# One tile shape for scores, projections and turns in a masked attention kernel: even key chunks, a padding row, and the output matmuls together

## The chip, the cores and the metric

The kernel runs on one core of a Trainium2 chip. The metric is the device time of one execution in microseconds (us), the median of several runs. The profile comes from one further execution; its span runs from the first to the last recorded instruction. Engines are called PE (TensorE, matrix products), ACT (ScalarE), DVE (VectorE), POOL (GpSimd) and SP (SyncE, which issues transfers here). Each engine and each queue works through its instructions in the order in which the program gives them.

## The reference

```python
def _L0_cond_ref(x, mask, Wq, Wo):          # x (8, 512, 1024), mask (8, 1024) of 0 and 1
    B, D, T = x.shape                       # NH = 8 heads, dk = 64
    xt = jnp.transpose(x, (0, 2, 1))
    q = xt @ Wq.T
    qh = q.reshape(B, T, NH, dk).transpose(0, 2, 1, 3)
    scores = scale * jnp.einsum('bhqd,bhkd->bhqk', qh, qh)   # queries are keys and values too
    logits = (scores * cmask + (1.0 - cmask) * NEG) * rmask
    attn = jax.nn.softmax(logits, axis=-1)
    ctx = jnp.einsum('bhqk,bhkd->bhqd', attn, qh)
    out = ctx.transpose(0, 2, 1, 3).reshape(B, T, D) @ Wo.T
    return jnp.transpose(out, (0, 2, 1))

x = x + _L0_cond_ref(x, cond_2048, Wq, Wo)
```

A masked key gets no weight. A masked query has all logits 0, so its context is the mean of all values, the same for every such query of a batch.

## The kernel before

Everything is fp32. `early()` counts the kept tokens of each batch and ranks them. If every batch keeps fewer than `NK` = 576 of its 1024 tokens, `late()` runs on the kept tokens alone; it is what the profile shows. `attention_of_all_tokens` is the way out for other inputs and does not run.

For each of 8 batches the tokens are turned to rows and stored in DRAM (`turn`, tile `xd`), a search over the ranks finds the rows of the kept ones (`search`), POOL gathers them in five tiles of up to 128 rows (`gather`, tile `xin`), and PE turns them back to feature-major columns (`collect`, tile `xc`, 512 features in `ND` = 4 blocks of 128 by 576 columns). The last column holds the batch's mean (`put_mean`), which stands for all masked queries.

The work then goes by *pairs* of heads: 4 pairs a batch, 32 in all, numbered p = 4 b + pr. For a pair: `project` makes the queries `qT` (128 rows, 64 a head) in two halves of 288 tokens; `values` turns them into `v`, squares them on ACT and reduces to a bound on the scores (`top`, then `bias_of`); `scores(pair, c)` makes, for key chunk c, the products of 128 keys with two halves of 288 queries and two heads, each head on its own 64 rows of the array, and ACT's exponential puts them in `e`; `add_up` sums each row of `e` over the valid columns on DVE, one masked reduction for each head (queries and keys are the same vectors, so a key's row sum is the softmax sum of that token as a query); `attend` multiplies `v` with `e` over the keys, into `av`, which ACT copies to `cT`; `invert`, a store and a broadcast load (`row`, `rb`, on SP) and `contexts` divide by the sums. 576 tokens are four key chunks of 128 and one of 64; for that last chunk the four products (two heads, two query halves) lie on four tiles of 64 x 64, and its sums come in two parts that `sum_last` adds. `output` multiplies four pairs' `cT` with `woT`, five token tiles a batch, ACT copies, POOL stores to `od`; `fetch` gathers rows of `od` back to the places of all tokens (8 indirect transfers on POOL), and `finish_blocks` turns them on DVE and adds `x`, which `load_rest` has loaded. SP stores the result. The last batch goes a shorter way (`begin_output`, `end_output`, `fetch_last`, `finish_tokens`).

The order is written out by hand. In pair p the loop runs over five chunks: `scores`, then the previous chunk's `add_up`, then whatever `slots_of` and the tables name for that pair and chunk: the projection of pair p + 2 in two lumps of 8 matmuls, the bias of pair p + 1, the values of pair p + 2 in the last slot, the outputs of the previous batch in slots 0 to 2 of pair 1, the mean and `collect` in slots 1 to 3 of pair 2. `attend` follows the loop. POOL's order within a steady batch is: output stores (pair 1, slots 0 to 2), five gathers (pair 1, slot 3), eight fetches (pair 2, slot 0). Eight of the features' sums for the mean stand on ACT in the chunks of pairs 0 and 1 (`add_features`).

PSUM tiles rotate: score tiles `s` of two banks, two of them, and tiles `t` of one bank, four of them (`bank`), for everything else. A new tile waits until the one that it replaces has been read.

Of the kernel before, what the change touches and what calls it, by code (L numbers as in the profile page):

```python
# [28 lines left out]

# [289 lines left out]
def attention_of_kept_tokens(ctx, tc, x, mask, wq, wo, out, ident, wqT, woT, verdict, flag):  # L319

# [36 lines left out]
    sizes = [min(P, NK - c * P) for c in range(-(-NK // P))]  # L357
    NC = len(sizes)
    LAST = NC - 1
    assert sizes[LAST] == DK == P // 2  # L360
    W = NC * P

# [5 lines left out]
    count = keep.tile([P, NK], F32, name="count")  # L368
    quadrant = keep.tile([P, A], F32, name="quadrant")
    within = keep.tile([P, Q], F32, name="within")  # L370
    key = keep.tile([P, NC], F32, name="key")
    kept = keep.tile([P, B], F32, name="kept")
    origin = keep.tile([P, B, NT], I32, name="origin")
# [3 lines left out]
    pens = keep.tile([P, B, NC], F32, name="pens")  # L377
    low = keep.tile([P, 2, LAST], F32, name="low")
    lowest = keep.tile([P, DK], F32, name="lowest")
    sums = [keep.tile([P, 2, NC], F32, name=f"sums_{i}") for i in range(2)]  # L380
    ris = [keep.tile([P, Q], F32, name=f"ris_{i}") for i in range(2)]
    ranks = dr.tile([B * NT, P], F32, name="ranks", bufs=1)

    def bank(name):
        return ps.tile([P, NB], F32, tag="t", name=name, bufs=4)
# [3 lines left out]
    xs, xbars, xmeans, xds, xins, xcs, valids, searches = {}, {}, {}, {}, {}, {}, {}, {}  # L389
# [13 lines left out]
    def queries_of(b):  # L403

        valid = sb.tile([P, NK], F32, tag="valid", name=f"valid_{b}")
        nc.gpsimd.tensor_scalar(valid, count, kept[:, b : b + 1], None, ALU.is_lt)  # L406
        part = sb.tile([P, KH], F32, tag="part", name=f"part_{b}")
        for r in range(2):
            rows = slice(r * DK, (r + 1) * DK)
            nc.gpsimd.tensor_copy(part[rows, :], valid[rows, r * KH : (r + 1) * KH])  # L410
        valids[b] = valid, part

    def turn_first(i):

        r, at = divmod(i * P, NB)
        pt = bank(f"xt_0_{i}")
        for d in range(ND):
            nc.tensor.transpose(pt[:, d * P : (d + 1) * P], xs[0][r][:, d, at : at + P], ident)  # L418
        if i == 0:
            xds[0] = dr.tile([T, D], F32, tag="xd", name="xd_0")  # L420
        tag = "oc" if i < NC else "xin"
        xt = sb.tile([P, D], F32, tag=tag, name=f"xt_0_{i}", bufs=NC)
# [11 lines left out]
    def turn(b, i):  # L434

        n = T // NQ
        r, at = divmod(i * n, NB)
        if i == 0:
            xds[b] = dr.tile([T, D], F32, tag="xd", name=f"xd_{b}")
# [34 lines left out]
    def place_ranks(b):  # L480
        rank = sb.tile([P, T], F32, tag="rank", name=f"rank_{b}", bufs=1)
        found = sb.tile([P, NC], F32, tag="found", name=f"found_{b}")
        source = sb.tile([P, NC], I32, tag="source", name=f"source_{b}")
        searches[b] = rank, found, source
# [8 lines left out]
    def search(b, i):  # L493

# [11 lines left out]
            source[:, col], found[:, col], float(i * P), float(T - 1), ALU.add, ALU.min  # L506
        )

    def gather(b, i):
# [3 lines left out]
        xin = sb.tile([P, D], F32, tag="xin", name=f"xin_{b}_{i}", bufs=NC)  # L513
# [8 lines left out]
    def collect(b, i):  # L522
        n = sizes[i]
        xin = xins[b][i]
        pt = bank(f"xc_{b}_{i}")
        for d in range(ND):
            nc.tensor.transpose(  # L527
                pt[:, d * n : (d + 1) * n], xin[:n, d * P : (d + 1) * P], ident[:n, :n]
            )
        m = min(n, NK - 1 - i * P)  # L530
        nc.scalar.copy(
            xcs[b][:, :, i * P : i * P + m],
            pt[:, : ND * n].rearrange("p (d n) -> p d n", d=ND)[:, :, :m],
        )

    def put_mean(b):

        xcs[b] = sb.tile([P, ND, NK], F32, tag="xc", name=f"xc_{b}", bufs=1)
        pm = bank(f"mean_{b}")
        for d in range(ND):  # L540
            nc.tensor.matmul(
                pm[d * Q : (d + 1) * Q, :A], within, xmeans[b][:, d, :], start=True, stop=True
            )
        nc.vector.tensor_scalar(xcs[b][:, :, NK - 1], pm[:, :A], 1.0 / T, None, ALU.mult)


    qTs, vs, tops, biases = {}, {}, {}, {}

    def project(pair, hf):
        b, pr = pair  # L550
        nm = f"{b}_{pr}"
        if hf == 0:
            qTs[pair] = sb.tile([P, W], F32, tag="qT", name=f"qT_{nm}", bufs=4)
        qT = qTs[pair]
        cols = slice(hf * KH, (hf + 1) * KH)
        pq = bank(f"pq_{nm}_{hf}")
        for d in range(ND):
            nc.tensor.matmul(  # L558
                pq[:, :KH],
                wqT[:, d, pr * P : (pr + 1) * P],  # L560
                xcs[b][:, d, cols],
                start=(d == 0),
                stop=(d == ND - 1),
            )
        nc.scalar.copy(qT[:, cols], pq[:, :KH])  # L565
        if hf == 1:
            nc.scalar.copy(qT[:, NK:W], pq[:, KH - DK : KH])

    def values(pair):
        nm = "%d_%d" % pair  # L570
        qT = qTs[pair]
        v = sb.tile([P, NC, P], F32, tag="v", name=f"v_{nm}", bufs=4)
        for at, n in ((0, LAST), (LAST, 1)):
            pt = bank(f"v_{nm}_{at}")
            for i in range(n):
                c = at + i
                nc.tensor.transpose(  # L577
                    pt[:, i * P : (i + 1) * P], qT[:, c * P : (c + 1) * P], ident
                )
            nc.scalar.copy(  # L580
                v[:, at : at + n, :], pt[:, : n * P].rearrange("p (c d) -> p c d", d=P)
            )
        vs[pair] = v
        sq = sb.tile([P, NC, P], F32, tag="sq", name=f"sq_{nm}", bufs=1)
        nc.scalar.activation(sq, v, AF.Square)  # L585
        lengths = sb.tile([P, 2 * NC], F32, tag="len", name=f"len_{nm}")
        nc.vector.tensor_reduce(  # L587
            lengths,
            sq.rearrange("p c (h d) -> p (c h) d", h=2),
            axis=AX.X,  # L590
            op=ALU.add,
        )
        tops[pair] = sb.tile([P, 1], F32, tag="top", name=f"top_{nm}")
        nc.vector.tensor_reduce(tops[pair], lengths, axis=AX.X, op=ALU.max)

    def bias_of(pair):
# [3 lines left out]
        nc.tensor.transpose(pt[:, :P], tops.pop(pair).to_broadcast([P, P]), ident)  # L600
        m = sb.tile([P, 1], F32, tag="m", name=f"m_{b}_{pr}")
        nc.vector.tensor_reduce(m, pt[:, :P], axis=AX.X, op=ALU.max)
        nc.vector.tensor_scalar(m, m, -SCALE, None, ALU.mult)  # L603
        biases[pair] = sb.tile([P, NC], F32, tag="bias", name=f"bias_{b}_{pr}")
        nc.vector.tensor_scalar(biases[pair], pens[:, b, :], m, None, ALU.add)

# [3 lines left out]
    def scores(pair, c):  # L610
        qT, nm = qTs[pair], "%d_%d_%d" % (*pair, c)
        heads = [slice(h * DK, (h + 1) * DK) for h in range(2)]
        keys = slice(c * P, c * P + sizes[c])
        if c < LAST:
            e = sb.tile([P, 2, 2, KH], F32, tag="e", name=f"e_{nm}", bufs=6)
        else:
            e = sb.tile([P, 1, 2, KH], F32, tag="el", name=f"el_{nm}")
            s = ps.tile([P, 2, NB], F32, tag="s", name=f"s_{nm}")
        for hf in range(2):
            queries = slice(hf * KH, (hf + 1) * KH)  # L620
            to = slice(0, P)
            if c < LAST:
                s = ps.tile([P, 2, NB], F32, tag="s", name=f"s_{nm}_{hf}")
            else:
                to = slice(hf * DK, (hf + 1) * DK)
            for h in range(2):
                nc.tensor.matmul(  # L627
                    s[to, h, :KH], qT[heads[h], keys], qT[heads[h], queries], start=True, stop=True
                )
            if c < LAST or hf == 1:  # L630
                nc.scalar.activation(  # L631
                    e[:, hf if c < LAST else 0, :, :],
                    s[:, :, :KH],
                    AF.Exp,
                    bias=biases[pair][:, c : c + 1],
                    scale=SCALE,
                )
        es[pair, c] = e

    def add_up(pair, c):  # L640

        b, pr = pair
        valid, part = valids[b]
        e = es[pair, c]
        for h in range(2):
            junk = sb.tile([P, T], F32, tag="junk", name=f"junk_{b}_{pr}_{c}_{h}", bufs=1)
            n = NK if c < LAST else KH
            nc.vector.tensor_tensor_reduce(  # L648
                junk[:, :n].rearrange("p (f k) -> p f k", k=KH),
                e[:, :, h, :],  # L650
                (valid if c < LAST else part).rearrange("p (f k) -> p f k", k=KH),
                1.0,
                0.0,
                ALU.mult,
                ALU.add,
                sums[pr % 2][:, h, c : c + 1],
            )

    def weigh(pair, av, c, hf):
        v, e = vs[pair], es[pair, c]  # L660
# [630 lines left out]
```

## Time and profile before

| what | us |
|---|---|
| median of 3 runs (807.15 to 809.01) | 807.57 |
| span of the profiled execution | 724.6 |
| first score starts, in the span | 37.0 |
| steady batch (batches 2 to 6) | 82.96 |
| last pair starts, in the span | 665.2 |
| last batch's tail, from the last output product's end to the end of the span | about 25 |
| ACT busy in the span | 384.1 |
| DVE busy in the span | 542.0 |
| POOL busy in the span | 171.9 |

The profiled execution's own time is its span and what lies around it; the runs differ from the span by 83.0 us (807.57 - 724.6), which is outside all recorded instructions. PE's mean granted clock is 0.98 of full speed. In the profile's rows, "128\*64" behind a matmul is the part of the array that it takes (rows\*columns), the rest are shapes of its operands; one fp32 product is two MATMUL instructions. "<-" names what ended an engine's idle time.

### The profile page before, as it was taken

To read this page: it belongs to the slowest core of one execution; us is meant where nothing else is said; L and a number is where in the kernel's file an instruction comes from. 1 tells how busy PE (TensorE), PEld (TensorE's weight loads), DVE (VectorE), ACT (ScalarE), POOL (GpSimd) and SP (SyncE) were. 2 spreads that over 40 slices of the span, in tenths; PEclk is the share of its full clock that TensorE was granted. 3 is DMA by queue.
4 is the path that set the end of the run, shared out by engine and by line. 5 is a ranking of instruction groups with operands and counts; after the bars stand their busy time and mean duration, and the time that the engine had idled before them with its cause. 6 is when DMAs were issued, how large, how long until landed. Compare 5 with 4: busy or idle time off the path is not lost.

```text
span 724.6 us, 11742 instructions
## 1 busy us (share of the span) xinstructions
PE 673.4 (93%) x4027; PEld 378.0 (52%) x4027; DVE 542.0 (75%) x1568; ACT 384.1 (53%) x763; POOL 171.9 (24%) x208
## 2 busy tenths in 40 slices
PE   6699999999999999999999999999999999998973
PEld 5555555555554555546554555455554555554332
DVE  6269967758986799858986699858988598637862
ACT  5476567455654556445664657445673645445300
POOL 4721000062102601054101701044100710023021
PEclk9899999999999999999999999999999999999985
DMA  8544152772579636783579634785468821754238
GB/s 292 157 150 129 56 164 64 185 196 93 181 199 234 201 96 181 209 207 124 164 193 229 200 125 142 206 222 152 164 169 199 215 88 41 167 132 131 59 113 248
DMA packets 96405, 117.35 MB, mean 162 GB/s; under 512 B 10080, under 2 KB 73632, under 8 KB 96336
## 3 DMA queue, kind: packets, MB, share of 16 engines
q1 hardware_dynamic: 79584, 74.14, 38.9%
q0 software_dynamic: 12528, 40.28, 17.8%
q10 hardware_dynamic: 4224, 2.10, 1.0%
q8 instruction: 33, 0.54, 0.3%
q14 instruction: 36, 0.29, 0.1%
HBM read 73.30 MB, written 43.18 MB: 161 GB/s over the span
## 4 chain that ended last, share of the span: by engine, by line
PE 82%; DVE 7%; ACT 6%; DMA 3%; issue 2%; POOL 0%; SPq 0%; DVEq 0%; POOLq 0%
PE av L664 19%; PE s L627 19%; PE pq L558 17%; PE po L777 15%; ACT e L631 4%; PE v L577 3%; PE xc L527 2%; DVE junk L648 2%; PE pa L797 2%; DVE junk L502 1%; DMA g<-od,origin 1%; PE xt L418 1%; DMA rb<-row 1%; PE po L813 1%; PE top L600 0%
## 5 line engine op out<-in xcount | busy, mean ns | idle before, releaser
L648 DVE CUSTOM_DVE_ANT_0 junk<-e,valid 128x576 f32<-128x576 f32 x256 | 193.5, 756 | 68.3 <-ACT e L631 61.3
L627 PE MATMUL s<-qT 64*128 64x288 f32 (+1 forms) x1280 | 186.7, 434 | 16.9 <-ACT e L631 16.7
L631 ACT ACTIVATE e<-s,bias 128x576 f32<-128x576 f32 x256 | 175.5, 737 | 20.4 <-PE s L627 17.2
L627 PEld LDWEIGHTS s<-qT 64*128 64x128 f32 (+1 forms) x1280 | 91.7, 174 | 103.9 <-ACT e L631 50.2
L558 PE MATMUL pq<-xc,wqT 128*128 128x288 f32 x512 | 140.4, 418 | 0.0
L664 PE MATMUL av<-e,v 128*64 128x288 f32 x1024 | 135.8, 411 | 0.1
L558 PEld LDWEIGHTS pq<-xc,wqT 128*128 128x128 f32 x512 | 92.2, 190 | 40.9 <-ACT cT L680 8.5
L777 PE MATMUL po<-woT,cT 128*128 128x512 f32 (+1 forms) x336 | 113.4, 525 | 0.0
L664 PEld LDWEIGHTS av<-e,v 128*64 128x64 f32 x1024 | 69.6, 136 | 55.0 <-ACT v L580 8.3
L786 POOL DMA_DIRECT2D od<-oc x42 | 23.4, 557 | 276.0 <-ACT oc L784 276.0
L777 PEld LDWEIGHTS po<-woT,cT 128*128 128x128 f32 (+1 forms) x336 | 48.9, 172 | 56.0 <-issue 51.5
L680 ACT COPY cT<-av 128x288 f32<-128x288 f32 x62 | 21.7, 402 | 97.7 <-PE av L664 97.7
L879 POOL DMA_INDIRECT g<-od,block_origin x56 | 62.1, 1109 | 19.0 <-issue 14.3
L784 ACT COPY oc<-po 128x512 f32<-128x512 f32 (+1 forms) x35 | 19.0, 543 | 87.0 <-PE po L777 85.7
L565 ACT COPY qT<-pq 128x288 f32<-128x288 f32 x64 | 25.5, 398 | 63.8 <-PE pq L558 63.8
L514 POOL DMA_INDIRECT xin<-xd,source x40 | 42.4, 1060 | 43.8 <-DVE m L603 25.6
L406 POOL TENSOR_SCALAR valid<-count,kept 128x576 f32<-128x576 f32 x8 | 14.1, 1762 | 130.3 <-DVE sums L648 130.2
L447 DVE STREAM_TRANSPOSE xt<-x 128x1024 f32<-128x1024 f32 x28 | 34.7, 1240 | 11.0 <-DMA xd<-xt 10.9
L587 DVE TENSOR_REDUCE len<-sq 128x10 f32<-128x640 f32 x32 | 25.8, 806 | 21.3 <-ACT sq L585 21.3
L502 DVE TENSOR_SCALAR_CACHE_REDUCE junk<-rank,key 128x1024 f32<-128x1024 f32 (+4 forms) x40 | 39.7, 994 | 1.5 <-ACT rank L1046 1.5
L849 DVE TENSOR_TENSOR xr<-o,xr 128x512 f32<-128x512 f32 x56 | 38.8, 692 | 1.9
L846 DVE STREAM_TRANSPOSE o<-g 128x512 f32<-128x512 f32 x56 | 39.3, 701 | 0.0
(139 smaller groups left out, 630.5 us busy)
## 6 DMA issues: line engine op xcount, KB each, us to landing
x<-in_x_dram SPq DMA_DIRECT2D x56, 256.0 KB
xd<-xt SPq DMA_DIRECT2D x112, 128.0 KB
xr<-in_x_dram SPq DMA_DIRECT2D x28, 512.0 KB
out_dram<-xr SPq DMA_DIRECT2D x24, 512.0 KB
rb<-row SPq DMA_DIRECT2D x60, 160.0 KB
od<-oc POOLq DMA_DIRECT2D x28, 256.0 KB, 4.0
rank<-ranks SPq DMA_DIRECT2D x6, 512.0 KB
xd<-xt POOLq DMA_DIRECT2D x8, 256.0 KB, 3.8
```

Source lines behind the costliest of these rows:

```text
L447: nc.vector.transpose(xt.rearrange("p k (d f) -> p k d f", d=ND), xs[b][r][:, :, at : at + n].rearrange("p d (k t) -> p k d t", t=Q),)
L502: nc.vector.tensor_scalar(junk[:, :n], rank[:, i * P :], key[:, col], 0.0, ALU.is_le, ALU.add, accum_out=found[:, col])
L514: nc.gpsimd.indirect_dma_start(out=xin[:n, :], out_offset=None, in_=xds[b], in_offset=bass.IndirectOffsetOnAxis(ap=searches[b][2][:n, i : ...
L558: nc.tensor.matmul(pq[:, :KH], wqT[:, d, pr * P : (pr + 1) * P], xcs[b][:, d, cols], start=(d == 0), stop=(d == ND - 1),)
L627: nc.tensor.matmul(s[to, h, :KH], qT[heads[h], keys], qT[heads[h], queries], start=True, stop=True)
L631: nc.scalar.activation(e[:, hf if c < LAST else 0, :, :], s[:, :, :KH], AF.Exp, bias=biases[pair][:, c : c + 1], scale=SCALE,)
L648: nc.vector.tensor_tensor_reduce(junk[:, :n].rearrange("p (f k) -> p f k", k=KH), e[:, :, h, :], (valid if c < LAST else part).rearrange(" ...
L664: nc.tensor.matmul(av[head, :KH], v[keys, c, head], e[keys, hf if c < LAST else 0, h, :], start=(c == 0), stop=(c == LAST),)
L777: nc.tensor.matmul(po[k * n : (k + 1) * n, :w], cTs[b, pr][:, i * P : i * P + n], woT[:, pr, k * w : (k + 1) * w], start=(pr == 0), stop=( ...
L846: nc.vector.transpose(o.rearrange("p k t -> p (k t)"), gs[b, i])
L849: nc.vector.tensor_tensor(to, o, to, ALU.add)
L879: nc.gpsimd.indirect_dma_start(out=g, out_offset=None, in_=ods[b], in_offset=bass.IndirectOffsetOnAxis(ap=block_origin[:, b, i : i + 1], a ...
```

## The change

What it does, by parts:

- Five even key chunks of N = 116 (577 columns and zero pads to W = 580) take the place of four of 128 and one of 64. The mean moves to column 576, a zero row is added to `xd`, and places beyond the kept tokens read that row. All sums then cover the zero columns too, and `inverses` subtracts their known part (`shift` times `unused`), so that the masked sums become plain reductions over both heads, and `sum_last` goes.
- The projection of pair p + 2 is cut into 8 steps of two matmuls with 64 features each (`project_units`), on the two row halves of the array, each half on another half of the tokens, and after four steps the halves change over. Turns of values, tops, gathered tokens and weights take 64-row halves too.
- The loop has ten slots (chunk and query half) with one projection step in eight of them; the values of pair p + 1 are in slot 4, its bias in slot 9.
- Output matmuls of a batch follow `attend` of the next batch's pair 0 in one stretch; `collect` follows `attend` of pair 1.
- `bank` gives two tiles of two banks; copies to SBUF are made for two banks at once. `fetch` moves to pair 1, chunk 1, `load_rest` to pair 0, chunk 2, `finish_blocks` to (1, 4) to (3, 1).

```diff
     def bank(name):
-        return ps.tile([P, NB], F32, tag="t", name=name, bufs=4)
+        return ps.tile([P, 2, NB], F32, tag="t", name=name, bufs=2)
...
+    def turn_split(pt, blocks):
+        for j, block in enumerate(blocks):
+            n = block.shape[0] // 2
+            for r in range(2):
+                rows = slice(r * DK, r * DK + n)
+                nc.tensor.transpose(
+                    pt[:, r, j * n : (j + 1) * n], block[rows, :], ident[rows, r * DK : r * DK + n]
+                )
...
+    def project_units(pair):
+        b, pr = pair
+        opened = []
+        def step(swap, d):
+            if not opened:
+                place_queries(pair)
+                opened.append(bank("pq_%d_%d" % pair))
+            pq = opened[0]
+            for r in range(2):
+                hf = r ^ swap
+                n = spans[hf].stop - spans[hf].start
+                nc.tensor.matmul(
+                    pq[:, hf, :n],
+                    wqT[halves[r], d, pr * P : (pr + 1) * P],
+                    xcs[b][halves[r], d, spans[hf]],
+                    start=(swap == 0 and d == 0),
+                    stop=(swap == 1 and d == ND - 1),
+                )
+            if swap and d == ND - 1:
+                for hf in range(2):
+                    keep_queries(pair, pq, hf)
+        return [lambda swap=swap, d=d: step(swap, d) for swap in range(2) for d in range(ND)]
...
     def values(pair):
+        pt = bank(f"v_{nm}")
+        for c in range(NC):
+            for h in range(2):
                 nc.tensor.transpose(
+                    pt[:N, h, c * DK : (c + 1) * DK],
+                    qT[halves[h], c * N : (c + 1) * N],
+                    ident[halves[h], halves[h]],
                 )
+        nc.scalar.copy(v[:N].rearrange("p h c d -> p h (c d)"), pt[:N, :, : NC * DK])
...
     def add_up(pair, c):
-            nc.vector.tensor_tensor_reduce(
...
+        nc.vector.tensor_reduce(
+            sums[pair[1] % 2][:N, :, c],
+            es[pair, c][:N].rearrange("p h f k -> p h (f k)"),
...
     def weigh(pair, av, c, hf):
+        keys = slice(0, min(N, NK - c * N))
         for h in range(2):
             nc.tensor.matmul(
+                av[halves[h], hf, :KH], v[keys, h, c, :], e[keys, h, hf, :],
...
+    def outputs(b, i, count, done):
+        po = bank(f"po_{b}_{i}")
+        for t in range(2):
+            for pr in range(count):
+                nc.tensor.matmul(po[:, t, :], cTs[b, pr][:, (i + t) * P : (i + t + 1) * P], woT[:, pr, :],
...
+        done(po)
...
+    def fills_of(p):
+        todo = [[] for _ in range(2 * NC)]
+        if p == 2:
+            for d in range(ND):
+                todo[d].append(lambda d=d: turn_weights(woT, "wo", d))
+        elif p + 2 < len(pairs):
+            steps = project_units(pairs[p + 2])
+            for i, step in enumerate(steps):
+                todo[i if i < ND else i + 2].append(step)
+        if p + 1 < len(pairs):
+            todo[4].append(lambda: values(pairs[p + 1]))
+            todo[2 * NC - 1].append(lambda: bias_of(pairs[p + 1]))
...
+    def interlude(p):
+        if pr == 0 and b > 0:
+            output_end(b - 1)
+            for i in (0, 2):
+                outputs(b - 1, i, ND, store_outputs(b - 1, i))
+        if pr == (1 if b else 2) and b + 1 < B:
+            for i in range(NG):
+                collect(b + 1, i)
+        if p == 2:
+            project(pairs[4])
...
+        FINISH = [(1, 4), (2, 0), (2, 1), (2, 2), (2, 3), (2, 4), (3, 0), (3, 1)]
+        def beside(p, c):
...
+                if pr == 1 and c == (3 if b else LAST):
+                    for i in range(NG):
+                        gather(b + 1, i)
...
+            if pr == 0 and c == 2 and b > 0:
+                load_rest(b - 1)
+            if pr == 1 and c == 1 and b > 0:
+                fetch(b - 1)
...
+            fills = fills_of(p)
+            for k in range(2 * NC):
+                c, hf = divmod(k, 2)
+                scores(pair, c, hf)
+                if hf == 1:
+                    beside(p, c)
+                for task in fills[k]:
                     task()
+                if hf == 1:
+                    issue_stores()
+            if pr == (1 if b else 2) and b + 1 < B:
+                put_mean(b + 1)
             if p + 1 < len(pairs):
                 attend(pair)
+            interlude(p)
```

More of the change, by code (lines that the diff above doesn't have):

```diff
@@ L544, in put_mean @@
[L544 to L567 removed]
+        for j in range(2):
+            for k in range(2):
+                nc.tensor.matmul(
+                    pm[halves[k], 0, :A],
+                    spot[:, j, :],
+                    xmeans[b][:, 2 * k + j, :],
+                    start=(j == 0),
+                    stop=(j == 1),
+                )
@@ L592, in values @@
         )
-        tops[pair] = sb.tile([P, 1], F32, tag="top", name=f"top_{nm}")
-        nc.vector.tensor_reduce(tops[pair], lengths, axis=AX.X, op=ALU.max)
-    def bias_of(pair):
-        b, pr = pair
-        pt = bank(f"top_{b}_{pr}")
[L600 to L605, printed above, removed]
@@ L608, in attention_of_kept_tokens @@
-    es, rbs, cTs = {}, {}, {}
[L610 to L638, printed above, removed]
```

566 lines of the change are left out of this document (290 added, 276 removed).

## The prediction, made before the changed kernel was run

> **What bounds it now.** I read the page's busy times and its chain first, then the stretches of one steady batch (batch 5; four feature pairs, one stretch each), then TensorE's timeline in such a batch, then the rows of the engines that feed it.
>
> ```profile
> PE 673.4 (93%) x4027; PEld 378.0 (52%) x4027; DVE 542.0 (75%) x1568; ACT 384.1 (53%) x763; POOL 171.9 (24%) x208
> ...
> PE 82%; DVE 7%; ACT 6%; DMA 3%; issue 2%; POOL 0%; SPq 0%; DVEq 0%; POOLq 0%
> ```
>
> TensorE (PE) is the bound: 93% busy, 82% of the chain.
>
> ```profile
> core 0: us, PE busy (x) PEld busy (x) DVE busy (x) ACT busy (x) POOL busy (x), PEclk, DMA share, GB/s
> 440.24:456.40 16.16, 15.45 (x108) 8.89 (x104) 15.39 (x44) 12.05 (x27) 0.87 (x2) 1.00 0.52 132
> 456.40:487.90 31.50, 31.14 (x153) 15.76 (x152) 21.83 (x70) 13.76 (x28) 7.79 (x10) 1.00 0.83 211
> 487.90:506.90 19.00, 18.34 (x135) 10.91 (x131) 14.41 (x37) 11.48 (x22) 9.67 (x9) 1.00 0.53 160
> 506.90:523.20 16.30, 15.58 (x106) 8.73 (x102) 15.50 (x43) 9.21 (x17) 1.80 (x1) 1.00 0.55 183
> ```
>
> A batch is 82.96 us. Pair 1 is long because it holds the output matmuls (15 us), and under them ScalarE (ACT, 13.76 us) has ample cover. Pair 2 holds the gathered tokens' turns.
>
> ```profile
> 284.41 0.71 PE L627 MATMUL s<-qT 64*64 64x288 f32 x8 [0.36 <-ACT e L631]
> 285.06 0.77 PE L577 MATMUL v<-ident,qT 128*128 128x128 f32 x5
> 285.75 4.10 PE L664 MATMUL av<-e,v 128*64 128x288 f32 x32
> 289.78 0.72 PE L664 MATMUL av<-el,v 64*64 64x288 f32 x8
> 290.43 1.24 PE L627 MATMUL s<-qT 64*128 64x288 f32 x8
> 291.60 2.21 PE L558 MATMUL pq<-xc,wqT 128*128 128x288 f32 x8
> 293.64 3.60 PE L777 MATMUL po<-woT,cT 128*128 128x512 f32 x8
> ```
>
> Each line has another array shape (64\*64, 128\*128, 128\*64, 64\*128). In the records of single matmuls, a pass over 288 columns starts 242 ns after the last of its shape (512 columns: 429 ns), two passes make one fp32 product, and two or four products on separate tiles start within 7 ns. A change of shape adds 91 ns to the pass before it and 35 to 104 ns to the first one after it: 0.19 us. The lines show it: the scores' four passes take 1.17 (290.43 to 291.60) where 4 x 0.242 = 0.97.
>
> **PE's own sum per steady batch.** Before: scores 4 pairs x 9 slots (the half chunk's four tiles run at once) x 0.485 = 17.5; contexts the same, 17.5; projections 4 x 8 x 0.485 = 15.5; outputs 4 x 4 x 0.859 + 8 x 0.215 = 15.5; turns (value, top, token; 109 ns each of 128 columns) 4.6. That is 70.6; 42 changes of shape x 0.19 = 8.0; 82.96 leaves 4.4 of waits.
> After: five chunks of 116 keys are five full slots for each token half, so scores and contexts are 10 slots a pair each, 19.4 + 19.4; projections 4 x 8 x 0.491 (292 columns) = 15.7, if the two 64-row halves run together as the scores' two rows do; outputs 15.5; turns, now two of 64 columns side by side, 2.8 (62 ns for a 64-column turn, the row of the last token tile; between 1.4 and 5.6 if they share less or more). Changes of shape: into the contexts and back in each pair, one more for the outputs: 9 x 0.19 = 1.7. Sum 74.5. PE's own work so falls by 4.0 a batch: 6.3 from changes and 1.8 from turns against 4.1 more for the two slots. **It gains only while its waits stay under 4.4 + 4.0 = 8.4 us a batch, 1.0 us a pair above today's.**
>
> **The waits after.** These rows price them:
>
> ```profile
> L631 ACT ACTIVATE e<-s,bias 128x576 f32<-128x576 f32 x256 | 175.5, 737 | 20.4 <-PE s L627 17.2
> ...
> L565 ACT COPY qT<-pq 128x288 f32<-128x288 f32 x64 | 25.5, 398 | 63.8 <-PE pq L558 63.8
> ...
> L587 DVE TENSOR_REDUCE len<-sq 128x10 f32<-128x640 f32 x32 | 25.8, 806 | 21.3 <-ACT sq L585 21.3
> ```
>
> Back to back, exponentials start 0.63 us apart, 288-column copies 0.30, the square of 640 columns 0.64, a feature sum with its read-out 0.61; a 640-column copy is 0.57 by the 512- and 288-column copies.
> (a) *Chunk 3.* The values' copy and square now stand on ACT between the two exponentials of chunk 2. From the start of the first, the second ends after 0.63 + 0.74 (the copy to its end) + 0.64 + 0.74 = 2.75. There are two score tiles. From the end of chunk 2's first scores PE has the turns, 0.31, and a score, 0.49; the next needs the first exponential's end, 0.2 + 0.74 + 0.1 = 1.04, and waits 0.25; a score and a projection step later, at 2.02, the next needs 0.2 + 2.75 + 0.1 = 3.05, and waits 1.03: 1.3.
> (b) *The top.* PSUM tiles are now two of two banks each. The projection's tile is open from slot 0 to 9, the values take the other, so the top's turn, in order on PE, waits for both qT copies, which stand behind the last exponential: from the last score's end 0.2 + 0.63 + 0.3 + 0.4 + 0.1 = 1.63, of which the last projection step fills 0.49: 1.1. Before, four one-bank tiles let this pass.
> So an ordinary pair (pair 3) is 4.85 + 3.93 + 0.31 + 0.2 in the stretch, + 1.3 + 1.1, + 5.05 contexts = 16.8, against 16.3.
> (c) *Pair 0* adds five feature sums to ACT: from the first score 0.7 + 6.3 (exponentials) + 1.4 + 3.1 + 0.8 = 12.3, with its gaps about 12.9, where PE has 9.3; with the contexts 17.9; then the outputs, 1.72 + 0.2 + 13.74: 33.6. ACT idles under these, since they now follow the contexts and no score needs it. Before, pair 0's work and the outputs took 16.16 + 31.50 less pair 1's own 16.
> (d) *Pair 1* is the largest term. The fetch of the previous batch's output rows is moved ahead of this batch's gathers on POOL, which issues in order:
>
> ```profile
> L514 POOL DMA_INDIRECT xin<-xd,source x40 | 42.4, 1060 | 43.8 <-DVE m L603 25.6 <-issue 7.6 <-DVE source L505 5.5
> ...
> od<-oc POOLq DMA_DIRECT2D x28, 256.0 KB, 4.0
> ```
>
> From pair 1's start: the last output copy (1024 columns, 1.0 by the copies) ends at 1.15; its store lands 4.0 later at the earliest, 5.2 (a store of twice the size: up to 6.5). Eight fetches then take 8 x 1.27 to 1.42 (the spacing in POOL's timeline) = 10.2 to 11.2, to 15.4 to 17.7; five gathers, the last issued 5.1 to 5.7 later and landing 4.0 on: 24.5 to 27.4. The collects that need them now stand in PE's order behind pair 1's contexts, free at 9.3 + 3.0 + 5.1 = 17.4, and all later scores behind them. Also in that order, the contexts' tile is the top's (the mean takes one in between) and waits for VectorE's maximum, queued behind the first finish, which waits for the first fetch: about 16.8; the gathers end later, so this adds nothing. I take 25.9 for the pair; before, the gathers went first and 10 us lay between them and their use.
> (e) *Pair 2* is 16.9: the collects left it.
> Batch after: 33.6 + 25.9 + 16.9 + 16.8 = 93.2, +10.2; six such batches, **+61**. Batch 0 has no outputs or fetch; its third pair does collects, weight turns and a whole projection in a row: 17.8 + 17.3 + 16.8 and 7.2 of stretch work, 3 of waits, 5.1 + 3 + 3.9 + 2 more behind ACT for the third: 76, against 71.6, the ends 3 apart from it: **+5**. Batch 7, up to its last pair: two pairs +2, the third, with no projections, 13.4 against 11.7 by ACT: **+3**. Before the first score a half projection is added, 8 x 0.242 = **+2**. The last pair and the end: 2 slots and fewer changes, four small VectorE steps and three finishes less ahead of the flag: 0 to -4, **-2**.
> Sum +69. The span 724.6 becomes 794. Runs are 807.57 at the median, 83.0 around the span that nothing here touches: **876 us**.
>
> What lies beside: the chunk sums on VectorE are five reductions of 1152 columns, 1.35 each by the reductions of 640 and 2048 (0.81, 2.28), against 7.4 a pair: less, off the path; uncovered it would be a gain of 0.5. The zero row is one small SP store a batch; the residual's load, four issues in 2.9 us, goes ahead of the token stores on SP, whose last land about 12 us into pair 1, before POOL gets to the gathers; if that cover went, 3 us a batch. The memset, token and unused edits are under 0.5 us, once or on POOL.
>
> The Trainium skill (TensorEngine Tiling (Array Packing), PSUM Bottleneck) says that tiling speeds up the array and not the emptying of PSUM, which may then bind, and asks for both ScalarE and VectorE there; (a) and (b) are that case, with all copies still on ACT.
>
> **Rivals.**
> 1. *Faster: PE's sum decides.* The place is ACT's queue in a pair: by sums (6.3 + 1.3 + 0.6 = 8.3 against PE's 9.3) it fits, and if exponentials, copies and gathers stay as hidden as today, waits stay at 4.4: 4.1 less in seven batches, 779. It decides below 8.4 us of waits a batch. Against: order, not sum, makes (a), (b) and (d). 9%.
> 2. *One of the two kinds of wait is missing.* Without (d), pair 1 ends by 20.6 to 23.2, 2.7 to 5.3 less: 844 to 860. Without (b), PE is 18 to 27 lower in all: 849 to 858. 17%.
> 3. *The clock falls.* The stretch from 19.3 to 26.1, after a 7.8 us idle of PE, has a granted clock of 0.50. Pair 1's waits add up to about 9 us; one 6.8 us stretch at 0.5 in six batches is + 20: 896. For it: the size; against: the waits come in pieces, the longest near 4. 8%.
> The skill (TensorE: Matmul & The Clock Gate, Part 1) puts the drop at one idle window of about 3.4 us; by it the 4 us piece could suffice.
> 4. *The projection halves take turns*, so that the change does not do what it says: 3.9 a pair, some 2.4 of it in the place of waits, over 29 pairs: 920 to 990. The scores, same shape, starting within 7 ns, speak against it. 4%.
> The forecast's case, 858 to 894: 62%.
>
> Within 0.2% (1.6 us, about what a measurement of this kernel can tell) lies almost nothing of these: 1%, from between 1 and 2; slower 90%. The range, 840 to 898, takes in the forecast, most of 2 and 3, and leaves rival 1 and 4 out.
>
> **What would show it.** Right: fewer than 100 changes of shape; the matmuls' idle time released by qT copies, one near 1.1 us in each pair; PE waiting for gathers behind pair 1; batches of 90 to 96 us; ACT idle under the outputs. Wrong: batches under 83, the top's turn starting at once, gathers landed before the contexts end, or projection steps of 0.98.

## The result and the profile after

| | kernel before | changed kernel |
|---|---|---|
| median, same series (4 runs each) | 808.09 us | 851.99 us (849.15 to 853.17) |
| ratio, 95% interval | | 1.0529 (1.0495 to 1.0562) |
| span of the profiled execution | 724.6 us | 849.6 us |
| that execution's own time | not given | 851.31 us: span + 1.7 |

The change makes the kernel 5.3% slower. A second series of the same pair gave 854.71 against 805.68 us, ratio 1.0595 (1.0534 to 1.0655). The forecast, 876 us, has the right sign and its range holds the time, but by luck: the profiles show that two large errors in it cancelled.

The unchanged kernel took 806 to 810 us in three series of runs made side by side (those of the table and series 1 and 3 below) and 728 us in two (series 2 and 4), and the profiled execution of before, span 724.6, was of the second kind, so that each kernel is compared only with the runs of the kernel before in its own series.

The page of the changed kernel, busy times and chain:

```profile
PE 700.2 (82%) x4843; PEld 427.9 (50%) x4843; DVE 481.4 (57%) x895; ACT 399.0 (47%) x716; POOL 138.2 (16%) x184
...
PE 55%; ACT 19%; DVE 15%; issue 7%; DMA 2%; SPq 1%; POOL 1%; POOLq 0%; DVEq 0%
```

PE's share of the chain fell from 82 to 55%: ACT and DVE now stand in it. The stretches of one steady batch (batch 3, pairs 0 to 3; columns as in the first such view):

```profile
334.94:368.33 33.39, 30.85 (x174) 16.97 (x172) 15.65 (x26) 14.49 (x29) 1.85 (x3) 1.00 0.80 197
368.33:395.76 27.43, 21.00 (x168) 12.90 (x167) 16.52 (x34) 14.04 (x27) 14.22 (x15) 0.88 0.57 170
395.76:412.69 16.93, 15.27 (x128) 10.46 (x128) 12.28 (x17) 9.79 (x16) 0.00 (x0) 1.00 0.01 2
412.69:430.40 17.71, 14.93 (x126) 9.94 (x124) 14.70 (x30) 9.92 (x17) 0.00 (x0) 1.00 0.62 196
```

The batch is 95.46 us; the forecast had 33.6, 25.9, 16.9 and 16.8, together 93.2. Pair 1 has a granted clock of 0.88. What ended PE's waits, over the whole span (us in total, times, longest):

```profile
PE av L664 <- DVE m L626: 42.0, 16, 5.6
PE s L640 <- ACT e L647: 32.2, 52, 2.3
PE av L664 <- ACT qT L541: 13.8, 12, 1.5
```

Before, the first kind of wait did not exist and the second was 16.7 us.

### The profile page after: what moved, and what is told of

Read it like the earlier page. It is cut to its first block, busy times and chain, and to the rows that moved or that the text cites. A ratio compares the mean times of both kernels' runs of the same rounds, so it can differ in the third digit from the quotient of the medians.

```text
span 849.6 us, 12592 instructions
## 1 busy us (share of the span) xinstructions
PE 700.2 (82%) x4843; PEld 427.9 (50%) x4843; DVE 481.4 (57%) x895; ACT 399.0 (47%) x716; POOL 138.2 (16%) x184
## 4 chain that ended last, share of the span: by engine, by line
PE 55%; ACT 19%; DVE 15%; issue 7%; DMA 2%; SPq 1%; POOL 1%; POOLq 0%; DVEq 0%
PE av L664 21%; PE po L773 13%; PE s L640 8%; ACT e L647 8%; DVE sums L653 6%; PE pq L580 5%; ACT junka L447 3%; ACT sq L610 2%; ACT v L605 2%; DVE junk L481 2%; PE pq L551 2%; DVE len L612 2%; PE po L801 1%; DVE cT L759 1%; PE xc L384 1%
## 5 line engine op out<-in xcount | busy, mean ns | idle before, releaser
L653 DVE TENSOR_REDUCE sums<-e 116x2 f32<-116x1152 f32 x160 | 213.2, 1345 | 207.5 <-ACT e L647 207.5
L640 PE MATMUL s<-qT 64*116 64x288 f32 x1280 | 230.6, 425 | 33.9 <-ACT e L647 32.2
L647 ACT ACTIVATE e<-s,m 116x576 f32<-116x576 f32 x320 | 231.2, 737 | 38.8 <-PE s L640 31.7
L664 PE MATMUL av<-e,v 116*64 116x288 f32 (+1 forms) x1280 | 192.6, 458 | 61.2 <-DVE m L626 42.0
L664 PEld LDWEIGHTS av<-e,v 116*64 116x64 f32 (+1 forms) x1280 | 101.3, 154 | 143.7 <-DVE m L626 45.8
L640 PEld LDWEIGHTS s<-qT 64*116 64x116 f32 x1280 | 113.2, 177 | 103.2 <-ACT e L647 70.7
L580 PE MATMUL pq<-xc,wqT 64*128 64x288 f32 (+1 forms) x928 | 159.2, 406 | 0.0
L773 PE MATMUL po<-woT,cT 128*128 128x512 f32 x248 | 109.0, 597 | 0.0
L580 PEld LDWEIGHTS pq<-xc,wqT 64*128 64x128 f32 x928 | 96.4, 188 | 23.4 <-ACT qT L541 0.2
L773 PEld LDWEIGHTS po<-woT,cT 128*128 128x128 f32 x248 | 46.5, 191 | 58.4 <-issue 57.9
```

The source lines that it names most:

```text
L580: nc.tensor.matmul(pq[:, hf, :n], wqT[halves[r], d, pr * P : (pr + 1) * P], xcs[b][halves[r], d, spans[hf]], start=(swap == 0 and d == 0), ...
L640: nc.tensor.matmul(s[:N, h, :KH], qT[halves[h], c * N : (c + 1) * N], qT[halves[h], hf * KH : (hf + 1) * KH], start=True, stop=True,)
L647: nc.scalar.activation(es[pair, c][:N, :, hf, :], s[:N, :, :KH], AF.Exp, bias=biases[pair][:N], scale=SCALE)
L653: nc.vector.tensor_reduce(sums[pair[1] % 2][:N, :, c], es[pair, c][:N].rearrange("p h f k -> p h (f k)"), axis=AX.X, op=ALU.add,)
L664: nc.tensor.matmul(av[halves[h], hf, :KH], v[keys, h, c, :], e[keys, h, hf, :], start=(c == 0), stop=(c == LAST),)
L773: nc.tensor.matmul(po[:, t, :], cTs[b, pr][:, (i + t) * P : (i + t + 1) * P], woT[:, pr, :], start=(pr == 0), stop=(pr == count - 1),)
```

## The 83 us "around the span"

*The kernel before, profiled again* (series 1; nothing changed).

> The kernel before, unchanged, profiled again. The profile of before has a span of 724.6 us while its runs take 807 to 809; the changed kernel's span (849.6) is within 2 us of its run (851.3). If something outside the recorded instructions takes 83 us in before, its span stays near 725 and its run near 808. If that profiled execution differed from the timed ones, the span of the timed executions is near 806, at a lower granted clock or with longer waits, and the steady batch is about 93 us instead of 83.

Measured: 810.2 us, ratio 1.0006 (0.9976 to 1.0036), and a span of 808.2 us for the execution's 810.01. Only 1.8 us lie around the span, so that the 83 us lie inside. The stretches of a steady batch:

```profile
299.71:315.81 16.10, 15.39 (x108) 8.85 (x104) 15.21 (x43) 12.05 (x27) 0.87 (x2) 1.00 0.56 136
315.81:347.31 31.50, 31.14 (x154) 15.77 (x150) 21.89 (x70) 13.77 (x28) 7.85 (x10) 1.00 0.84 210
347.31:378.71 31.40, 21.94 (x134) 12.75 (x130) 15.87 (x46) 12.16 (x22) 9.14 (x9) 0.78 0.31 97
378.71:395.11 16.40, 15.68 (x108) 8.79 (x104) 14.20 (x34) 9.23 (x17) 1.80 (x1) 1.00 0.55 181
```

Pairs 0, 1 and 3 are those of the first profile to 0.1 us. Pair 2 is 31.40 us in place of 19.00. Over batches 1 to 6 and the shorter pair 2 of batch 7 this is 83.1 us: all of the 83.

The timeline at the start of that pair (in brackets the idle time before, and what ended it):

```profile
347.32 1.24 PE L627 MATMUL s<-qT 64*128 64x288 f32 x8
...
350.88 0.74 ACT L631 ACTIVATE e<-s,bias 128x576 f32<-128x576 f32 x1 [1.03 <-remote]
...
351.68 1.19 PE L627 MATMUL s<-qT 64*128 64x288 f32 x4 [3.11 <-ACT e L631]
352.53 0.96 POOL L879 DMA_INDIRECT g<-od,block_origin  x1 [0.30 <-issue]
353.79 0.96 POOL L879 DMA_INDIRECT g<-od,block_origin  x1 [0.30 <-issue]
354.64 0.74 ACT L631 ACTIVATE e<-s,bias 128x576 f32<-128x576 f32 x1 [3.02 <-remote]
```

By the trace both score tiles of chunk 0 were computed by 348.56 (347.32 + 1.24; the ends of matmuls are modelled), yet ACT began the second exponential at 354.64, after 3.02 us of idling. "Remote" names no instruction: the thing that ACT waited for was PE's completion signal itself. In the records each signalling matmul can be set beside the moment at which its signal was counted. The median is 0.43 us after the matmul's start in both profiles. In the first profile none of 665 came later than 1.5 us. In the second some 45 of 658 did, the latest 8.4 us after the start (its trace has a few signals fewer than signalling matmuls, so that single pairings are uncertain). All but one or two at the very end lie while a row of POOL's indirect transfers was on its way: in the steady batches five gathers and eight fetches, issued 1.25 us apart (341.8 to 358.1 in this batch), with the late signals from 347.0 to 356.8, so from some 5 us after the first issue. In pair 1, with more traffic (210 GB/s), none was late until that row had begun in its last 5.5 us. While PE waited, its granted clock fell to 0.5, for 13.7 us in each of these pairs (10.2 in batch 7). In every one the first late signal belongs to a matmul that starts 3.8 to 5.2 us ahead of the fall (347.0 against 351.9 here), so that the clock is not what began it.

So the step "83.0 around the span that nothing here touches" was wrong. They lay inside, in a pair that the change rearranges.

## Experiments on the change's own parts

**The top's turn in a score tile** (series 1, kernel before 809.85 us):

```diff
     def bias_of(pair):
-        pt = bank(f"top_{b}_{pr}")
+        pt = ps.tile([P, 2, NB], F32, tag="s", name=f"top_{b}_{pr}")
```

> The changed kernel with the top's turn in a score tile, so that the two-bank tiles go projection, values, contexts. Theory (the waits at the shared two-bank tiles cost): contexts no longer wait for the copies of the queries or for the maximum, 1 to 2 us less in most pairs, 822 to 834 us. Rival (the two added slots and PE's own work cost it, waits would be covered): no change, 849 to 854.

Measured: 811.12 us, ratio to before 1.0024 (1.0002 to 1.0047): less time than either forecast. This one line is worth 40 us: span 849.6 to 809.4. A steady batch (batch 4):

```profile
407.83:439.66 31.83, 30.79 (x175) 16.96 (x173) 15.75 (x26) 14.50 (x29) 1.86 (x3) 1.00 0.83 224
439.66:467.06 27.40, 19.62 (x168) 12.86 (x167) 16.52 (x34) 14.04 (x27) 14.26 (x15) 0.91 0.60 180
467.06:483.63 16.57, 15.79 (x129) 11.40 (x128) 11.35 (x15) 9.93 (x16) 0.00 (x0) 0.95 0.00 1
483.63:500.03 16.40, 15.28 (x126) 9.60 (x125) 15.55 (x32) 9.83 (x17) 0.00 (x0) 1.00 0.50 152
```

The waits of `av` for `m`, 42.0 us, are gone. Against the changed kernel, batches 2 to 6 together are 12.7 us shorter; batch 0 gives 14.4, batch 1 7.9, batch 7 with the end 7.8 (the first score came 2.8 later). It is shown that the top's turn in the two shared PSUM tiles causes these waits. Pair 1 gained nothing by it (27.4 to 28.8 us in batches 1 to 6 against 27.2 to 28.4): its contexts no longer wait for `m`, but the clock still falls to 0.5 there.

**The fetch behind the gathers**, alone and together with the edit above (series 1):

```diff
-            if pr == 1 and c == 1 and b > 0:
+            if pr == 2 and c == 0 and b > 0:
                 fetch(b - 1)
...
-        FINISH = [(1, 4), (2, 0), (2, 1), (2, 2), (2, 3), (2, 4), (3, 0), (3, 1)]
+        FINISH = [(2, 2), (2, 3), (2, 4), (3, 0), (3, 1), (3, 2), (3, 3), (3, 4)]
```

> The changed kernel with the eight fetches back behind the gathers (pair 2, chunk 0) and the finishes three slots later. Theory (POOL's order holds the gathers and with them pair 1): pair 1 goes from 27.4 to 22 to 23.5 us, held then by the mean and the maximum, the clock stays at full speed there, 820 to 834 us. Rival (the collects wait for copies, not for gathers): pair 1 stays above 26 and the time above 845.

> Both edits. Theory: they add up, since pair 1 is held by both in turn: steady batch near 86 us, 795 to 815 us. Rival (the clock is what costs): only the batch's half-speed stretch goes, 3.4 us a batch, 825 to 835 as with either alone.

Measured: 898.29 us (1.1086 to before) and 850.78 (1.0499), both misses. The first added 46 us to the changed kernel where 18 to 32 should have gone; the second added 40 us to the kernel with the top's edit where between 16 less and 4 more were expected. The first one's waits:

```profile
ACT cT L679 <- remote: 80.3, 6, 14.5
```

Once a batch ACT idles some 13 us ahead of its copy of the contexts. Part of that is the contexts' own run; the signal of their last matmul came 6.9 to 8.5 us after its start, as the row's second half now lies over the end of the contexts. This is only a part of the 46 us. About half of what a steady batch lost stands in pair 0 (37.6 to 38.4 us against 33.4), where no signal was late: the contexts wait 4.0 us for `m` in place of 1.5 for `qT`, and the clock falls to 0.5 for 3.4 or 6.8 us behind that. In the run with both edits pair 0 lost 0.8 us and pair 1 most of the rest (33.7 to 34.5 us in batches 2 to 6), where PE waits 9.9 to 12.9 us for the copy of the contexts in these batches.

In the changed kernel the same row begins with the fetch at slot (1, 1) and is under way while PE runs the contexts, which need only one signal at their end; only some 19 signals of 561 were late. The move of the fetch that the prediction charged for thus seems to have spared the changed kernel most of what pair 2 pays in the kernel before. This is argued from where the signals lie. It fits that the two differ so little in a steady batch here (95.4 against 95.5) although each is some 12 us over the 83 of the first profile, the one by late signals, the other mostly by waits of its own.

**Moves of the fetch in the program order** (series 2, kernel before 727.71 us, no late signals): in the kernel before to pair 3; in the kernel before cut into four rows of two; in the changed kernel with the top's edit, cut by twos.

```diff
-                if pr == 2 and c == 0 and b > 0:
-                    fetch(b - 1)
+                if b > 0 and b + 1 < B and (pr, c) in FETCH:
+                    k = FETCH.index((pr, c))
+                    fetch(b - 1, range(2 * k, 2 * k + 2))
```

> The kernel before, with the eight indirect transfers of the fetch issued at the start of pair 3 in place of pair 2 (the finishes follow them), so that POOL no longer issues thirteen in a row (five gathers, eight fetches). Theory L (late signals): PE's completion signals reach ACT late while a long row of indirect transfers is moving; in the second profile of the kernel before they were up to 8.4 us late in pair 2, from 5 us after the row's first issue to its last landing, and that is the 12 us by which pair 2 (31.5 us) is longer than in the first profile (19.0). It expects pair 2 at 19 to 20 us and pair 3, which now has a row of eight beside it, at 16.3 to 24: batch 83 to 91 and 725 to 785 us in all. Rival H (half clock): pair 2 is long because the clock falls to half there for a reason of PE's own, and POOL's order has no part in it: pair 2 stays at 31 us, 805 to 815 us.

> The kernel before, with the fetch cut into four rows of two transfers, at slots (2, 1), (2, 3), (3, 0) and (3, 2). Theory L: no row is long enough to make signals late except the five gathers', whose last two lie at the start of pair 2; pair 2 at 19 to 22 us, pair 3 at 16.3 to 17, 725 to 750 us. Rival H: pair 2 stays at 31 us, 805 to 815 us. A third possibility, that every indirect transfer in flight delays the signals, whatever its company: pairs 2 and 3 share the 12 us, 790 to 815 us with no half of it gone.

> The changed kernel with the top's turn in a score tile and the fetch in four rows of two, (1, 1), (2, 0), (2, 2), (2, 4), finishes after them, load of x at (1, 2). Beside the run with the top's turn alone (811 us; pair 1 28.5, pair 2 16.5, pair 3 16.4). Theory L: with two transfers ahead of the gathers in place of eight, the gathers land some 7 us earlier, the collects start after contexts at full clock (4.9 us in place of 8.5), and no signal is late: pair 1 at 22 to 24 us, pairs 2 and 3 at 16.5: 770 to 785 us. Rival: fetches beside the scores of pair 2 cost as much as in the run with the fetch in pair 2 as one row (850 us): 830 to 855 us.

Measured: 793.07 us (ratio 1.0907, 1.0878 to 1.0937), 726.67 (0.9988, 0.9973 to 1.0002) and 799.72 (1.0987, 1.095 to 1.1023). The first two tell nothing on the late signals, as there were none to remove. The third, which also moves the load of `x` from (0, 2) to (1, 2), is between its two forecasts: two fetches went ahead of the gathers and six in a row behind them; pair 1 is 25.7 to 27.5 us, pair 2 17.6 to 18.3. The first is slower for a reason of its own: the later finishes put the output's stores on SP ahead of the token stores (SP at 318.29 and 324.18), the gathers follow these, and pair 2 waits (28.6 to 30.8 us in batches 2 to 6):

```profile
DVE rb L752 <- DMA rb<-row: 15.9, 1, 15.9
...
PE xc L527 <- DMA xin<-xd,source: 6.7, 1, 6.7
```

*By twos again* (series 3, kernel before 805.68 us, signals late):

> The kernel before with the fetch in four rows of two, once more, as on the first chip there were no late signals to remove (0 of 665 over 1.5 us late) and so nothing was tested. On a chip where the kernel before takes about 808 us, theory L (a long row of indirect transfers makes PE's signals late) expects pair 2 at 19 to 22 us in place of 31.5 and 725 to 760 us; the rival (half clock for a reason of PE's own) 805 to 815; a third (every transfer in flight delays the signals) 790 to 815. On a chip where the kernel before takes about 728 us: 727 us again.

Measured: 805.37 us, ratio 1.0001 (0.9976 to 1.0026), pair 2 at 27.6 to 31.9 us. These are the rival's numbers, but POOL's timeline shows that the edit moved nothing:

```profile
439.25 0.93 POOL L514 DMA_INDIRECT xin<-xd,source  x1 [0.30 <-issue]
440.48 0.96 POOL L879 DMA_INDIRECT g<-od,block_origin  x1 [0.30 <-issue]
441.74 0.95 POOL L879 DMA_INDIRECT g<-od,block_origin  x1 [0.30 <-issue]
```

POOL has nothing else to do there and runs ahead: thirteen in a row, whatever the place in the text. Nor does the rival hold by the order in time: in this trace too, late signals lie 3.7 to 5.9 us ahead of each fall of the clock in these pairs. A real delay needs a dependency: in series 4 (kernel before 728.02 us) the fetches' indices come through a small DVE copy at the wanted slot.

```diff
+            rows = sb.tile([P, NT], I32, tag="at", name=f"at_{b}_{part[0]}", bufs=2)
+            nc.vector.tensor_copy(rows[:, cols], block_origin[:, b, cols])
...
-                    ap=block_origin[:, b, i : i + 1], axis=0
+                    ap=rows[:, i : i + 1], axis=0
```

> The kernel before, with the fetch in four rows of two, and each row held back by a small DVE copy of its indices at slots (2, 1), (2, 2), (2, 4), (3, 1): POOL has nothing else to do there, so that the move in the program order alone had moved nothing (its trace shows thirteen transfers in a row again, 1.25 us apart). On a chip where the kernel before takes about 806 us: theory L (a long row of indirect transfers in flight makes PE's signals late) expects pair 2 at 19 to 23 us in place of 31.5, and 725 to 755 us; the rival (half clock for a reason of PE's own) 800 to 812; the third (every indirect transfer in flight delays the signals, whatever its company) 780 to 812, with the 12 us spread over pairs 2 and 3. On a chip where the kernel before takes about 728 us: 727 to 731.

Measured: 727.66 us, ratio 0.9993 (0.998 to 1.0006). The row is broken up:

```profile
405.11 0.93 POOL L514 DMA_INDIRECT xin<-xd,source  x1 [0.30 <-PE av L664]
409.11 1.38 POOL L884 DMA_INDIRECT g<-od,at  x1 [3.08 <-DVE xc L544]
...
418.43 0.95 POOL L884 DMA_INDIRECT g<-od,at  x1 [3.19 <-DVE at L881]
...
428.13 0.94 POOL L884 DMA_INDIRECT g<-od,at  x1 [7.50 <-DVE at L881]
```

But in this series' profiles no signal was late, here or in the next kernel, so that the theory stays untested: that the row makes the signals late is argued from where they lie, not shown.

**The same hold in the changed kernel with the top's edit** (series 4):

> The changed kernel with the top's turn in a score tile, and the fetch behind the gathers in four rows of two held back by DVE copies at (2, 0), (2, 1), (2, 3), (3, 0). It takes the fetch out of the gathers' way (the prediction's fourth wait: pair 1 at 25.9 us by the gathers' landing behind eight fetches) without a long row. Theory: the gathers are issued some 10 us earlier, land before the contexts end, and pair 1 falls from 28.5 to 21 to 24 us with contexts at full clock; pairs 2 and 3 stay within 1.5 us of 16.5: 765 to 790 us where the kernel before takes 806 (there the top's turn alone gave 811), 755 to 780 where it takes 728. Rival: pair 1 is bounded by its collects' copies and the mean alone, not by the gathers: 25 us and more, 795 to 815.

Measured: 791.29 us, ratio 1.0885 (1.0846 to 1.0924), 11 us over the forecast for such a series. Pair 1 is 23.2 to 24.6 us, as forecast (27.4 to 28.8 with the top's edit alone, in series 1); pairs 0 and 2, at 32.7 and 17.1 to 18.4, took some of it back. PE's contexts now take 5.05 us, and then PE does wait for the gathers, 19.5 us in the span:

```profile
PE xc L384 <- DMA xin<-xd,source: 19.5, 22, 2.1
```

This edit, too, moves the load of `x` from (0, 2) to (1, 2), which its forecast left out. SP issues the load at 435.15 in batch 4, just ahead of the gathers (438.30 to 443.39). The gathers land 8.7 us after their issue at the median, as in the run by twos (8.6), against 3.6 in the next run, whose load stays at (0, 2). That the load delays them is likely, but no run changes it alone.

**Pair 0's feature sums beside the outputs** (series 2, with the top's edit):

```diff
-                if pr < 2 and pr * NC + c < NN * ND:
+                if pr == 1 and NC + c < NN * ND:
...
+        if pr == 0 and b + 1 < B:
+            for i in range(NC):
+                add_features(b + 1, i)
```

> The changed kernel with the top's turn in a score tile, and pair 0's five sums of features (ACT, 0.63 + 0.20 us each) after attend, beside the outputs' matmuls, where ACT is idle, in place of the chunks. Theory (the prediction's third wait): the sums delay pair 0's exponentials; pair 0 falls from 31.8 us by 0.8 to 2, 6 batches: 811 to 799 to 806 us. Rival: pair 0's chunks are bounded by PE and the values' copy alone, the sums lie in ACT's gaps: pair 0 stays at 31.8 us, 809 to 813 us.

Measured: 795.39 us, ratio 1.093 (1.0903 to 1.0958). Its total can't be set beside the 811 of another series. Its pair 0 (batch 4) can be set beside that of the run by twos in the same series, 31.82 us with the sums in the chunks (31.83 in series 1):

```profile
395.43:426.73 31.30, 30.54 (x175) 17.10 (x173) 15.74 (x26) 11.86 (x19) 1.85 (x3) 1.00 0.83 220
```

The sums cost 0.5 us there, less than either end of the forecast's 0.8 to 2. Moved, they stand behind the output copies on ACT, run at the start of pair 1, and PE waits 4.0 us for exponentials there in place of 1.0.

**The changed kernel again** (series 3):

> The changed kernel, unchanged, once more. The kernel before took 808 to 810 us on one chip and 728 us on another, and its profiled execution of 724.6 us was of the second kind. If this run falls on a chip where the kernel before takes about 728 us, the prediction's steps, which were worked out from that profile, are tested without late signals: they gave a span of 794 us. From the pairs of the first profile of the changed kernel (start 48, batch 0 89, batch 1 98, five batches of 94.5 with contexts at full clock, end 122) I expect 825 to 840 us there. On a chip where the kernel before takes about 808 us: 849 to 854 again.

Measured: 854.71 us, near the second branch; most pairs repeat to 0.1 us, and pair 1 of batch 5, where signals came up to 8.6 us late, is 30.8 us against 27.9. It was not run where the kernel before takes 728 us, so the ratio there is open; the three variants run there were 8.9 to 9.9% slower. None of the variants of the changed kernel beats the kernel before.

## Why the prediction came out as it did

| term | predicted us | measured us |
|---|---|---|
| first score | 39.0 (37.0 + 2) | 48.4 |
| batch 0 | 76.6 | 89.3 |
| batch 1 | 92.9 | 101.6 |
| batches 2 to 6 | 5 x 93.2 = 466.0 | 478.7 |
| batch 7 and the end | 119.4 | 131.5 |
| span | 794 | 849.6 |
| around the span | 83.0 | 1.7 |

The forecast of the span was 56 us too low and the constant 81 too high. Of the signs that the prediction gave, three of the right ones came true (fewer than 100 changes of shape, batches of 90 to 96 us, ACT idle under the outputs), and two of the wrong ones did as well: the top's turn started at once, and the gathers landed before the contexts ended.

- **PE's own sum: right in kind, the gain too large.** Changes of shape fell from 346 to 93 in the recorded matmuls, 8 to 10 in a steady batch as forecast; a projection step's four passes lie side by side, 0.49 us (378.37 to 378.85 to 379.34 for score, step and top), so rival 4 is out. Counted from matmul start to matmul start in batch 3 (an estimate), PE's own work fell from 79.4 to 76.7 us, 2.7 in place of 4.0. Its waits rose from 3.5 to 15.3 us, and a stretch at half clock takes another 3.4.
- **(a) Chunk 3: right, a little large.** Waits of 0.28 and 0.75 us in pairs 0 and 1, and of 0.75 alone in pairs 2 and 3; forecast 0.25 and 1.03.
- **(b) The top: right in kind, wrong in place, too small.** The turn itself took the free tile at once, against "the top's turn waits"; the contexts' tile that follows is the one that waits, for the qT copies (0.9 to 1.5 us in pairs 2 and 0) or for DVE's maximum of the top's own turn (3.2 and 2.0 in pairs 1 and 3, up to 5.6 in batch 0). The forecast was 1.1 a pair, and "18 to 27 lower" without it; the run without it was 40 lower. This is most of what batches 0, 1 and 7 are over.
- **(c) Pair 0: right number, wrong parts.** It took 33.4 us against 33.6, but the sums are 0.5 of it (31.82 to 31.30) and (b) 1.6 (33.40 to 31.83).
- **(d) Pair 1: near in size, but the wait at its end is another.** The contexts start 16.44 us into the pair (forecast 16.8). Then:

```profile
379.34 0.22 PE L622 MATMUL top<-ident,top 64*128 64x64 f32 x2
381.21 0.40 PE L522 MATMUL mean<-mean,spot 128*64 128x4 f32 x8 [1.64 <-DVE mean L454]
384.77 8.45 PE L664 MATMUL av<-e,v 116*64 116x288 f32 x40 [3.16 <-DVE m L626]
393.15 0.46 PE L384 MATMUL xc<-ident,xin 64*128 64x64 f32 x8
```

  The contexts take 8.45 us where 5.05 were counted, as the granted clock is 0.5 from 383.8 to 390.6. The gathers, last issued at 389.94, land in that time (the last packet of their queue ends at 392.6, the contexts at 393.2), and PE never waits for them, although the forecast listed that as its sign. The fall of the clock is **rival 3**, and it came in every steady batch. The pair is 1.5 us over the forecast (27.4 against 25.9). That isn't the price of the clock: at full clock the contexts would have ended near 389.8, and PE would have met the gathers still on their way. The idle before it is 1.64 + 3.16 us with 0.40 of work between. The Trainium skill (TensorE: Matmul & The Clock Gate, Part 1) has the clock drop after one idle window of about 3.4 us. The stretches at 0.5 recorded here are 3.4, 6.8, 10.2 or 13.7 us long, apart from the last of each run, multiples of it, which agrees; but the 3.4 us ahead of the fall at 383.8 held 0.40 us of PE's work, so that such a window need not be wholly idle. Two slips of the prediction here move nothing: 8 x 1.42 is 11.4 and not 11.2, and its example of the clock, the stretch from 19.3, begins 4.3 us into the idle of 7.8 us and not after it.
- **Ahead of the first score: too small.** It is +11.4 against +2. About half comes from the same two tiles: the turns of batch 0's tokens wait for each other's copies (the rank products that follow start at 19.73 in place of 13.89). The half projection of the forecast's +2 is there too. The first score stays at 48.7 to 51.2 in all variants, so that this part of the loss was not removed by any.
- **The step that failed is "83.0 around the span that nothing here touches".** What lies around the span is 1.7 us. It was taken for overhead because it was in no record. It was the sign that the profiled execution was of another kind than the runs. With 1.7 in its place the forecast would have been 796 against a measured 808 for the kernel before, that is, the wrong sign; the right answer needed the other steps' shortfall of 56 us too. So the time in the range was luck, though the kinds of wait were mostly foreseen.

## What to carry to other kernels

Compare the span of a profile with the median of the runs first: if some per cent lie outside, the profile shows another execution, and no difference of stages may be added to the runs' median until a second profile says where the rest went. When PSUM tiles are made larger and fewer, list for each tile not only what its user waits for, but which tile the next allocation gets: here a turn of 0.2 us held up contexts of 5 us, and one line gave 40 us back. An engine with an empty queue runs ahead of the text: a transfer is delayed only by a dependency.

## What the runs showed of the hardware

PE's completion signals can reach the other engines up to 8.4 us after the matmul's start (kernel before; 0.43 at the median), up to 13.0 in the kernel with both edits of series 1, mostly while rows of 8 to 13 indirect transfers are on their way. ACT's own were counted 0.01 us after the instruction's end at the median, and at most one of 655 was more than 1 us late. The same rows went without a late PE signal in the profiles of series 2 and 4. Series 3, with late signals, and series 4, without, ran on one chip, so that it is not a property of a chip. What decides it stays open.
